# The first two attention steps of a Swin block written anew, and a convolution's pieces spread over four rounds

## The chip, the cores and the metric

The kernel runs on one core of a Trainium2 chip. The metric is the device time of one execution in microseconds (us), median of several runs. In the profile PE is TensorE, PEld its weight loads, DVE VectorE, ACT ScalarE, POOL GpSimd and SP SyncE, which only issues transfers.

## The reference

The input is 16 images of 192 channels and 56 x 56 pixels in f32. Two layers follow each other.

```python
# layer 0: a shifted-window attention block with an MLP, per image
h = layernorm(x over channels) * norm1_g + norm1_b
h = roll(h, (-3, -3))                       # then cut in 8 x 8 windows of 7 x 7
q, k, v = h @ qkv_w + qkv_b                 # 6 heads of 32 channels
p = softmax(q * 32**-0.5 @ k.T + rel_bias[REL_IDX] + window_mask)
x1 = x + roll_back(p @ v @ proj_w + proj_b)
y = gelu(layernorm(x1) @ fc1_w + fc1_b) @ fc2_w + fc2_b      # 192 -> 768 -> 192
x2 = x1 + y
# layer 1: a depthwise 3 x 3 convolution with weights made from the image itself
t  = relu(batchnorm(mean(x2 over pixels) @ w1.T))
wt = (t @ w2.T + b2) * MASK                 # of the nine taps four are not masked
out = depthwise_conv(x2, wt) + conv_bias
```

The weights of the convolution need the mean over the whole image, so it can begin only when the image's last MLP is done.

## The kernel before

A step is a quarter of an image: two bands of 7 rows, 16 windows (T = 392 pixels in a band). There are 64 steps. The kernel is software-pipelined by hand: the order written is the order on each engine. Round i (2 to 65) does the MLP of step i-2, the attention of step i, q, k and v of step i+1, and the sums for norms of steps i+2 (norm 1) and i-1 (norm 2). Steps 0 and 1 are done ahead of the rounds, in the part that is called the start here.

PSUM is taken as four pairs of banks (0 to 3), each one tile deep, so a pair is reused when the last reader of its tile is done:

```python
def banks(name, k):
    return psum.tile([128, 2, 512], F32, tag=f"pair{k}", name=name)
```

A norm is made as sums on TensorE (`st`, `singles`), a variance (`dev`), a root, a reciprocal, and then transfers that spread the result over partitions (`dv`):

```python
def norm_squares(key, i, side, engine):        # sq
    ...                                        # engine: ACT or GpSimd, two squares
    for h in range(2):
        nc.gpsimd.tensor_tensor(s0[p, h], s0[p, h], s1[p], ALU.add)

def norm_vars(keys):                           # dev <- st
    for s in sides:
        nc.scalar.activation(d[var[s]], stats[s][mean[s], :T], AF.Square)
    for s in sides:
        nc.vector.tensor_tensor(d[var[s]], stats[s][var[s], :T], d[var[s]], ALU.subtract)
...
def norm_devs(keys):
    part, d = norm_vars(keys)
    norm_root(part)                            # ACT, Sqrt
    table(AF.Gelu)                             # loads ACT's next table ahead
    nc.vector.reciprocal(part, part)
    return d
# norm_spread: dv <- dev, 8 transfers for a step; norm1_scale: win <- x * dv;
# norm2_scale: yn <- x * dv, on GpSimd
```

An attention step: scores (`sc`), `e` = scores + bias, a maximum, a subtraction, an exponential, a sum, a reciprocal, `prob` on GpSimd; then turns (`pt`, transposed on TensorE, copied to `prt` by ACT), values (`po`), rows (`o`), projection (`pp`) and residual (`x`). q, k and a mixed block e of both (`pq`, `pk`, `pe`) and v (`pv`) come from `win`; ACT copies q, k and e (`outs[0]` to `outs[3]`), DVE and ACT copy v into `vbd`.

The start, cut:

```python
... # loads of 7 rows of image 0, qkv weights, columns; then all other rows, mask, rel_bias
norm_squares("1_0", 0, 0, nc.gpsimd)
fold_scale(raw, g1, eff)
keys = stats_of(-2)                            # sums of step 0
pm = fold_means(eff, 3 * DIM, "fq", 0)
dvs.update(norm_spread(keys, norm_devs(keys), (nc.sync, nc.scalar)))
norm_squares("1_1", 1, 0, nc.gpsimd)
... # fold of qkv weights and biases; zeros into kbd, vbd, prob
keys = stats_of(-1)                            # sums of step 1
dev = norm_devs(keys)
norm1_scale(0, dvs.pop(0), nc.vector)
...
qs[0], outs = attention_qk(0, 1, 0, 2)
for f in outs:
    f()
... # image 1; proj and fc1 weights; bias_t
tail_of(-1, None, None, (2, 0))                # v of step 0
... # norm 2's parameters, fc2 weights

for i, extra in ((0, (proj_bias, mlp_weights)), (1, (taps_weights,))):
    top, share = attention_scores(i, *qs.pop(i), (1, 2, 0, 1))
    norm1_scale(i + 1, dvs.pop(0), nc.gpsimd)
    top(0)
    for wp in range(3):
        top(wp + 1)
        share(wp)
    share(3)
    qs[i + 1], outs = attention_qk(i + 1, 1, 0, 2)
    for f in outs:
        f()
    ...
    for e in extra:                            # parameters of later stages
        e()
    keys = stats_of(i)
    dev = norm_devs(keys)
    dvs.update(norm_spread(keys, dev))
    prts = [attention_turn(i, wp, wp % 2) for wp in range(4)]
    ...
    o = attention_rows(i, attention_values(i, prts, 0, 3))
    tail_of(i, o, 1, (2, 0))                   # projection, v of step i+1, residual, squares
```

The convolution of an image is six pieces (`conv_begin` on ACT, three taps on DVE in `conv_rest`, then transfers out). They are taken two in a round from the round after the image's last MLP on:

```python
for i in range(2, NS + 2):
    A, B_, C, D = pairs
    cs = conv_ready(2)
    ys = [conv_begin(*c) for c in cs[:1]]
    if has(i + 1):
        norm1_scale(i + 1, dvs.pop(0), nc.vector)
    def after():
        ys.extend(conv_begin(*c) for c in cs[1:])
        for c, y in zip(cs, ys):
            conv_rest(*c, y)
    if (i + 3) % STEPS == 0 and (i + 3) // STEPS < B:
        b = (i + 3) // STEPS
        images[b] = load_x(b, nc.sync)         # three image buffers
    def between():
        singles[0] = banks(f"st_{i}", C)
        keys.update(stats_of(i))
        var.append(norm_vars(keys))
    ...
    # ph <- yn, wf; after() runs after three of six blocks, between() after the next short ones
    mlp_first(i - 2, yns.pop(i - 2), hid, (A, B_, C, D, A, B_), after, between)
    ...
    if has(i):
        top, share = attention_scores(i, *qs.pop(i), (C, D, A, B_))
    ...
    # pf <- hid, wf, with turns, values, projection, v of step i+1, residual;
    # in each fourth round the taps of the image (taps, taps_hidden, taps_rows, taps_out)
```

Of the kernel before, what the change touches and what calls it, by code (L numbers as in the profile page):

```python
# [14 lines left out]
C0, C1 = 128, 64  # L15
# [21 lines left out]
def tile_swin_then_dynamic_conv(  # L37
# [48 lines left out]
    singles = [banks("singles", 3)]  # L86
# [44 lines left out]
    def columns(sources, tag, name, queue, k):  # L131


        n = sum(count for _, count in sources)
        rows = one.tile([n, 256], F32, tag=tag, name=f"{name}_rows")
        at = 0
        for src, count in sources:
            queue.dma_start(rows[at : at + count, 0:DIM], src.rearrange("(r c) -> r c", c=DIM))
            at += count
        nc.vector.tensor_copy(rows[:, DIM:256], rows[:, C0:DIM])  # L140
        pt = bank(k)
        for c in range(2):
            nc.tensor.transpose(
                pt[:, c * n : (c + 1) * n], rows[:, c * 128 : (c + 1) * 128], ident[:n, :n]
            )
        cols = const.tile([128, 2, n], F32, tag=name, name=name)
        nc.vector.tensor_copy(cols.rearrange("p c n -> p (c n)"), pt[:, 0 : 2 * n])
        return [(cols[:, 0, r : r + 1], cols[:, 1, r : r + 1]) for r in range(n)]
# [4 lines left out]
    def fold_scale(raw, g, dst):  # L153
        for c in range(2):
            nc.vector.tensor_scalar(dst[:, c], raw[:, c], g[c], None, ALU.mult)
# [58 lines left out]
    raw_all = one.tile([128, 2, 6 * DIM + HID], F32, tag="hid", name="raw")  # L214
    raw, eff = raw_all[:, :, 0 : 3 * DIM], raw_all[:, :, 3 * DIM : 6 * DIM]
    rawf = raw_all[:, :, 6 * DIM :]
# [24 lines left out]
    def norm_squares(key, i, side, engine):  # L241
# [9 lines left out]
        for h in range(2):  # L251
            p = slice(h * 64, h * 64 + 64)
            nc.gpsimd.tensor_tensor(s0[p, h], s0[p, h], s1[p], ALU.add)  # L253
# [22 lines left out]
    def norm_vars(keys):  # L276

        sides = sorted(keys)
        d = one.tile([128, T], F32, tag="dev", name=f"dev_{keys[sides[0]]}")
# [12 lines left out]
    def norm_devs(keys):  # L292

        part, d = norm_vars(keys)
        norm_root(part)
        table(AF.Gelu)
        nc.vector.reciprocal(part, part)
        return d

    def norm_spread(keys, d, queues=(nc.sync,)):  # L300

        out = {}
        for side in sorted(keys, reverse=True):
            tag = ("dv1", "sq01")[side]
            v = one.tile([128, 2, T], F32, tag=tag, name=f"dv_{keys[side]}")
# [40 lines left out]
    def norm2_scale(i, dv):  # L346
# [3 lines left out]
        nc.gpsimd.tensor_tensor(y0, v0, dv, ALU.mult)  # L350
        for h in range(2):
            p = slice(h * 64, h * 64 + 64)
            nc.gpsimd.tensor_tensor(y1[p], v1[p], dv[p, h], ALU.mult)
# [406 lines left out]
    def tail_of(i, o, kp, kv):  # L760

        pvs, v_rest, v_whole = attention_v(i + 1, kv) if has(i + 1) else (None, None, None)
        if o is not None:
            pp, pair1, narrow, rest, whole = project(i, o, kp, 3)
            narrow()
            rest()
        if pvs:
            v_rest()
        if o is not None:
            whole()  # L770
            residual(i, pp, pair1)
        if pvs:
            v_whole()
            attention_v_out(pvs)
        if o is not None:
            norm_squares(f"2_{i}", i, 1, nc.scalar)

# [3 lines left out]
    nc.vector.memset(pick, 0.0)  # L781
    for h in range(4):
        nc.vector.memset(pick[h * HD : (h + 1) * HD, h % 2 : h % 2 + 1], 1.0)
# [5 lines left out]
    nc.vector.memset(rel_r, 0.0)  # L789
    nc.vector.memset(wp2, 0.0)  # L790
    images[0] = new_x(0)
    load_rows(*images[0], 0, 0, WS, nc.sync)
    nc.scalar.dma_start(raw[:, 0], qkv_w[0:C0])
    rows2(raw[:, 1], qkv_w, nc.scalar)
    g1, be1, bq, bk, bv = columns(
        ((norm1_g, 1), (norm1_b, 1), (qkv_b, 3)), "q2", "cols1", nc.scalar, 0
    )
    load_rows(*images[0], 0, WS, 2 * WS, nc.sync)
    load_rows(*images[0], 0, 2 * WS, HALF, nc.sync)
    nc.sync.dma_start(mask_t, win_mask)  # L800
# [13 lines left out]
    nc.gpsimd.memset(win0, 0.0)  # L814
    nc.gpsimd.memset(win1, 0.0)
    norm_squares("1_0", 0, 0, nc.gpsimd)


    fold_scale(raw, g1, eff)
    keys = stats_of(-2)  # L820
    pm = fold_means(eff, 3 * DIM, "fq", 0)
    dvs.update(norm_spread(keys, norm_devs(keys), (nc.sync, nc.scalar)))
    norm_squares("1_1", 1, 0, nc.gpsimd)
    fold_center(eff, 3 * DIM, pm)
    for to, lo, n, s in (
        (0, 0, 128, SCALE),
        (128, DIM, 128, 1.0),
        (256, 128, 64, SCALE),
        (320, DIM + 128, 64, 1.0),
        (384, 2 * DIM, DIM, 1.0),  # L830
    ):
        nc.vector.tensor_scalar(
            wqkv[:, :, to : to + n], eff[:, :, lo : lo + n], s, None, ALU.mult
        )
    pq = bank(1)
    for c, at, lo, n, be, bias in (
        (0, 0, 0, 128, be1, bq[0]),
        (1, 0, DIM, 128, be1, bk[0]),
        (2, 0, 128, 64, be1, bq[1]),
        (2, 64, DIM + 128, 64, be1, bk[1]),  # L840
    ):
        p = slice(at, at + n)
        shift(pq[p, c : c + 1], raw, lo, n, be)
        nc.vector.tensor_tensor(qkb[p, c : c + 1], bias[p], pq[p, c : c + 1], ALU.add)
    nc.vector.tensor_scalar(qkb[:, 0:1], qkb[:, 0:1], SCALE, None, ALU.mult)
    nc.vector.tensor_scalar(qkb[0:64, 2:3], qkb[0:64, 2:3], SCALE, None, ALU.mult)
    nc.vector.tensor_scalar(kb, pick, qkb[:, 1:2], None, ALU.mult)
    for t in [kbd] + vbd + prob:
        nc.gpsimd.memset(t, 0.0)
    keys = stats_of(-1)  # L850
    dev = norm_devs(keys)
    norm1_scale(0, dvs.pop(0), nc.vector)
    dvs.update(norm_spread(keys, dev))
    norm_squares("1_2", 2, 0, nc.gpsimd)
    qs[0], outs = attention_qk(0, 1, 0, 2)
    for f in outs:
        f()
    images[1] = load_x(1, nc.sync)
    nc.gpsimd.dma_start(wp0, proj_w[0:C0])
    rows2(wp1, proj_w[:, 0:C0], nc.gpsimd)  # L860
    for h in range(2):
        p = slice(h * 64, h * 64 + 64)
        nc.gpsimd.dma_start(wp2[p, p], proj_w[C0:DIM, C0:DIM])
    nc.gpsimd.dma_start(rawf[:, 0], fc1_w[0:C0])
    rows2(rawf[:, 1], fc1_w, nc.gpsimd)
    rel_hk = rel_r[:, ::-1, :].rearrange("p k h -> p h k")
    for r in range(2):
# [14 lines left out]
    tail_of(-1, None, None, (2, 0))  # L882
    g2, be2, f2b, pb, cb = columns(
        ((norm2_g, 1), (norm2_b, 1), (fc2_b, 1), (proj_b, 1), (conv_bias, 1)),
        "sq11",
        "cols2",
        nc.gpsimd,
        0,
    )
    nc.gpsimd.dma_start(f1b, fc1_b.rearrange("(f p) -> p f", p=128))  # L890
    nc.gpsimd.dma_start(wf2, fc2_w.rearrange("(f p) n -> p f n", p=128))

    def proj_bias():

        pv = bank(1)
        for c, n in ((0, 128), (1, 64)):
            shift(pv[0:n, c : c + 1], raw, 2 * DIM + c * 128, n, be1)
            nc.vector.tensor_tensor(bv[c][0:n], bv[c][0:n], pv[0:n, c : c + 1], ALU.add)
        pv = bank(0)
        mm(pv[:, 0:1], wp0[:, 0:C0], bv[0], True, False)  # L900
        mm(pv[:, 0:1], wp1[0:64], bv[1][0:64], False, True)
        for h in range(2):
            p = slice(h * 64, h * 64 + 64)
            mm(pv[p, 1:2], wp0[:, C0:DIM], bv[0], True, False)
            mm(pv[p, 1:2], wp2[0:64, 0:64], bv[1][0:64], False, True)
        for c in range(2):
            nc.vector.tensor_tensor(pb[c], pb[c], pv[:, c : c + 1], ALU.add)

    def mlp_weights():
        fold_scale(rawf, g2, wf1)  # L910
        pm = fold_means(wf1, HID, "ff", 2)
        pf = bank(1)
        for f in range(NFC):
            shift(pf[:, f : f + 1], rawf, f * 128, 128, be2)
        fold_center(wf1, HID, pm)
        nc.vector.tensor_tensor(f1b, f1b, pf[:, :NFC], ALU.add)

    def taps_weights():

        w1n = one.tile([RED, 3, 64], F32, tag="prt", name="w1n", bufs=4)  # L920
        nc.gpsimd.dma_start(w1n, w1.rearrange("r (k c) -> r k c", c=64))
        w1d = one.tile([RED, 2, 64], F32, tag="prt", name="w1d", bufs=4)
        for h in range(2):
            nc.vector.tensor_copy(w1d[:, h], w1n[:, 2])
        pt = bank(0)
        nc.tensor.transpose(
            pt[:, 0:RED], w1n[:, 0:2].rearrange("r k c -> r (k c)"), ident[:RED, :RED]
        )
        nc.tensor.transpose(
            pt[:, 64 : 64 + RED], w1d.rearrange("r k c -> r (k c)"), ident[:RED, :RED]  # L930
        )
        nc.vector.tensor_copy(
            w1t, pt[:, 0:128].rearrange("p (k r) -> p k r", k=2)[:, :, 0:RED]
        )
        w2v = w2.rearrange("(c t) r -> c t r", t=9)[:, 0:NTAP, :]
# [238 lines left out]
```

## Time and profile before

| what | before |
|---|---|
| median of 3 runs | 3253.55 us (3251.41 to 3253.6) |
| span of the profiled run | 3251.8 us, mean granted TensorE clock 0.986 |
| PE busy | 3123.3 us (96%) |
| DVE busy | 2115.2 us (65%) |
| ACT busy | 1887.8 us (58%) |
| POOL busy | 991.6 us (30%) |
| chain that ended last | PE 85%, DVE 9%, issue 2%, POOL 1% |
| first MLP matmul (`ph`) of round 2 | 174.88 us |
| first MLP matmul of round 65, the last | 3195.77 us |

The page cuts the span in 40 slices of 81 us and gives the busy share of each engine in tenths; two slices hold the start. Windows of 20 us show it closer. Most matrix products go through one helper line (L92), so a product is known by its tiles' names: `ph` and `pf` are the MLP, `sc`, `pt`, `po`, `pp` attention, `pq`, `pk`, `pe`, `pv` q, k and v, `st` sums. The time from the first `ph` of a round to the first of the next is that round's time.

### The profile page before, as it was taken

To read this page: it belongs to the slowest core of one execution; us is meant where nothing else is said; L and a number is where in the kernel's file an instruction comes from. 1 tells how busy PE (TensorE), PEld (TensorE's weight loads), DVE (VectorE), ACT (ScalarE), POOL (GpSimd) and SP (SyncE) were. 2 spreads that over 40 slices of the span, in tenths; PEclk is the share of its full clock that TensorE was granted. 3 is DMA by queue.
4 is the path that set the end of the run, shared out by engine and by line. 5 is a ranking of instruction groups with operands and counts; after the bars stand their busy time and mean duration, and the time that the engine had idled before them with its cause. 6 is when DMAs were issued, how large, how long until landed. Compare 5 with 4: busy or idle time off the path is not lost.

```text
span 3251.8 us, 64181 instructions
## 1 busy us (share of the span) xinstructions
PE 3123.3 (96%) x26130; PEld 1937.1 (60%) x26130; DVE 2115.2 (65%) x3895; ACT 1887.8 (58%) x2988; POOL 991.6 (30%) x897
## 2 busy tenths in 40 slices
PE   5699999999999999999999999999999999999996
PEld 3556666666656656666666656666665665666653
DVE  5355675766766575685676666576676667667564
ACT  2455665655655665565565565565565666566552
POOL 5333233233223323323323323323323322322220
PEclk9699999999999999999999999999999999999998
DMA  3001011111111202112111201112111121211001
GB/s 99 16 15 51 25 37 51 37 55 31 40 52 32 60 31 61 31 31 56 36 52 40 58 26 40 51 35 56 31 37 55 31 59 32 61 30 32 22 30 45
DMA packets 79123, 135.35 MB, mean 42 GB/s; under 512 B 21766, under 2 KB 61692, under 8 KB 76908
## 3 DMA queue, kind: packets, MB, share of 16 engines
q1 hardware_dynamic: 77266, 128.54, 14.0%
q8 instruction: 206, 3.38, 0.4%
q0 software_dynamic: 1056, 1.92, 0.3%
q10 hardware_dynamic: 506, 0.79, 0.1%
q14 instruction: 89, 0.73, 0.1%
HBM read 41.25 MB, written 38.54 MB: 25 GB/s over the span
## 4 chain that ended last, share of the span: by engine, by line
PE 85%; DVE 9%; issue 2%; POOL 1%; ACT 0%; DMA 0%; SPq 0%; DVEq 0%; POOLq 0%; ACTq 0%
PE pf L92 23%; PE ph L92 19%; PE pp L92 7%; PE pv L92 6%; PE po L92 6%; PE pt L508 4%; PE pq L92 4%; PE sc L92 4%; PE pk L92 4%; PE pe L92 4%; PE st L92 3%; DVE y L708 3%; DVE win L339 1%; DVE vbd L451 1%; DVE x L584 1%
## 5 line engine op out<-in xcount | busy, mean ns | idle before, releaser
L92 PE MATMUL ph<-yn,wf 128*128 128x392 f32 (+1 forms) x3072 | 808.8, 501 | 9.3 <-ACT hid L598 3.5
L92 PE MATMUL pf<-hid,wf 128*128 128x392 f32 (+1 forms) x3072 | 802.8, 494 | 3.5 <-ACT hid L598 2.0
L495 POOL TENSOR_TENSOR prob<-e,tot 113x588 f32<-113x588 f32 x256 | 298.6, 1177 | 1205.6 <-DVE tot L494 1190.0
L92 PEld LDWEIGHTS ph<-yn,wf 128*128 128x128 f32 (+1 forms) x3072 | 424.7, 188 | 365.0 <-issue 83.9
L451 ACT COPY vbd<-pv 49x192 f32<-49x192 f32 x512 | 160.6, 314 | 704.2 <-DVE vbd L451 699.5
L92 PEld LDWEIGHTS pf<-hid,wf 128*128 128x128 f32 (+1 forms) x3072 | 386.3, 164 | 303.7 <-issue 120.0
L644 DVE SCALAR_TENSOR_TENSOR x<-pf,cols,x 128x784 f32<-128x784 f32 (+1 forms) x128 | 106.1, 829 | 537.8 <-PE pf L92 508.7
L598 ACT ACTIVATE hid<-ph,f1b 128x784 f32<-128x784 f32 x384 | 337.2, 913 | 115.1 <-PE ph L92 114.0
L253 POOL TENSOR_TENSOR sq<-sq,sq 64x392 f32<-64x392 f32 x256 | 263.7, 1030 | 369.5 <-ACT sq L247 354.9
L708 DVE SCALAR_TENSOR_TENSOR y<-x,wt,y 128x770 f32<-128x770 f32 x288 | 314.0, 1104 | 16.6 <-ACT y L693 8.4
L350 POOL TENSOR_TENSOR yn<-x,dv 128x784 f32<-128x784 f32 x64 | 119.0, 1859 | 571.3 <-DMA dv<-dev 549.1
L92 PEld LDWEIGHTS pv<-wqkv,win 64*128 64x128 f32 (+1 forms) x2048 | 258.1, 190 | 35.1 <-ACT kbd L405 2.8
L92 PE MATMUL pv<-wqkv,win 64*128 64x192 f32 (+1 forms) x2048 | 274.8, 327 | 3.3 <-ACT kbd L405 2.5
L486 DVE TENSOR_TENSOR e<-e,top 113x588 f32<-113x588 f32 x256 | 267.1, 1043 | 8.9
L92 PE MATMUL pp<-o,wp 128*128 128x392 f32 (+2 forms) x896 | 251.5, 514 | 2.7 <-ACT o L544 2.7
L489 ACT ACTIVATE e<-e 113x588 f32<-113x588 f32 x256 | 176.7, 691 | 132.9 <-DVE e L486 132.9
L238 ACT ACT_TABLE_LOAD x192 | 246.3, 1283 | 3.4
L514 ACT COPY prt<-pt 128x678 f32<-128x678 f32 x256 | 179.3, 727 | 117.2 <-PE pt L508 115.7
L479 DVE TENSOR_TENSOR e<-sc,bias_t 113x588 f32<-113x588 f32 x256 | 179.9, 763 | 100.5 <-PE sc L92 100.3
L508 PEld LDWEIGHTS pt<-ident,prob 113*128 113x128 f32 x1536 | 167.3, 142 | 77.8 <-issue 48.7
L92 PE MATMUL po<-prt,vbd 128*64 128x49 f32 x6144 | 199.9, 225 | 0.0
L92 PEld LDWEIGHTS po<-prt,vbd 128*64 128x64 f32 x6144 | 191.9, 140 | 9.4 <-ACT prt L514 0.6
(146 smaller groups left out, 3987.0 us busy)
## 6 DMA issues: line engine op xcount, KB each, us to landing
dv<-dev SPq DMA_DIRECT2D x1020, 49.0 KB
x<-in_x_dram SPq DMA_DIRECT2D x15, 1484.0 KB
out_dram<-y SPq DMA_DIRECT2D x48, 392.0 KB
out_dram<-y SPq DMA_DIRECT2D x48, 196.0 KB
x<-in_x_dram SPq DMA_DIRECT2D x16, 392.0 KB
x<-in_x_dram SPq DMA_DIRECT2D x15, 350.0 KB
out_dram<-y SPq DMA_DIRECT2D x16, 308.0 KB
out_dram<-y SPq DMA_DIRECT2D x16, 154.0 KB
```

Of the source, the lines that this page charges most:

```text
L92: nc.tensor.matmul(dst, lhs, rhs, start=start, stop=stop, skip_group_check=True)
L238: nc.scalar.activation(junk, eps_t[0:1], func)
L253: nc.gpsimd.tensor_tensor(s0[p, h], s0[p, h], s1[p], ALU.add)
L451: copy(dst, src[s * 64 : s * 64 + N, h, :, :, j, :])
L479: nc.vector.tensor_tensor(e, sc[:PW, :, : HEADS * N], rel, ALU.add)
L486: nc.vector.tensor_tensor(ehs[wp], ehs[wp], t.broadcast_to([PW, 2 * HEADS, N]), ALU.subtract)
L489: nc.scalar.activation(es[wp], es[wp], AF.Exp)
L495: nc.gpsimd.tensor_tensor(prob[wp][:PW, :, 0:N], ehs[wp], t.broadcast_to([PW, 2 * HEADS, N]), ALU.mult)
L508: nc.tensor.transpose(pt[:, a, g * PW : (g + 1) * PW], prob[wp][:PW, h : h + 2, :].rearrange("p h k -> p (h k)"), ident[:PW, :PW],)
L514: nc.scalar.copy(prt, pt[:, :, : 3 * PW])
L598: nc.scalar.activation(hid[:, f], phs[f][:, :, :T], AF.Gelu, bias=f1b[:, f : f + 1])
L708: nc.vector.scalar_tensor_tensor(dst, src, wt[:, kc, t : t + 1], dst, ALU.mult, ALU.add)
```

## The change

The start is written anew, straight and without the loop. It is to bring everything in order of need:

- parameter rows are loaded first on ACT's queue, fc1's weights follow the image on SyncE's, proj weights and norm 2's rows come early on GpSimd's; the taps' parameters are loaded in the start rather than when they are used;
- qkv weights are scaled straight into their place instead of through a copy; zeros go in on DVE early;
- squares of step 0 and 1 go to ACT, the adds of step 0 to DVE; steps 1 and 2 get their sums together, step 3 with norm 2 of step 0;
- v of step 0 follows q and k of step 0 at once; q and k of step 1 are issued before the maxima of step 0; the proj bias moves to the beginning, fc1's fold into step 0, fc1's shifts and the taps' parameters into step 1;
- ACT's tables are loaded ahead of need.

In the rounds, an image's six pieces are taken 1, 2, 2, 1 over four rounds instead of 2, 2, 2 over three, and in round 64 `yn` is made half by DVE. The order of bank pairs is named otherwise.

```diff
-    singles = [banks("singles", 3)]
+    singles = [None]
...
-    def norm_squares(key, i, side, engine):
+    def norm_squares(key, i, side, engine, adder=None):
...
-            nc.gpsimd.tensor_tensor(s0[p, h], s0[p, h], s1[p], ALU.add)
+            (adder or nc.gpsimd).tensor_tensor(s0[p, h], s0[p, h], s1[p], ALU.add)
...
+    table(AF.Sqrt)
+    g1, be1, bq, bk, bv = columns(*rows1, 2)
+    norm_squares("1_0", 0, 0, nc.scalar, nc.vector)
+    fold_scale(raw, g1, wqkv, (...))
+    singles[0] = banks("st_a", 3)
+    keys = {0: "1_0"}
+    norm_stats(keys, {0: 0})
+    part, dev = norm_vars(keys, "o")
+    norm_root(part)
+    nc.vector.reciprocal(part, part)
+    dvs.update(norm_spread(keys, dev, (nc.sync, nc.scalar)))
+    pm = fold_means(wqkv, 3 * DIM, "fq", 0)
+    fold_center(wqkv, 3 * DIM, pm)
...                                            # qkv biases
+    norm_squares("1_1", 1, 0, nc.scalar)
+    norm_squares("1_2", 2, 1, nc.gpsimd)
+    singles[0] = banks("st_b", 3)
+    keys = {0: "1_1", 1: "1_2"}
+    norm_stats(keys, {0: 1, 1: 2})
...                                            # norm 2's columns, proj bias
+    part, dev = norm_vars(keys)
+    norm_root(part)
+    norm1_scale(0, dvs.pop(0), nc.vector)
+    nc.vector.reciprocal(part, part)
...                                            # rel_bias, mask, spread, image 1
+    norm_squares("1_3", 3, 0, nc.gpsimd)
...                                            # loads of later parameters
+    qs[0], outs = attention_qk(0, 1, 2, 3)
+    pvs, v_rest, v_whole = attention_v(0, (0, 1))
+    v_rest()
+    v_whole()
+    table(AF.Exp)
+    for f in outs:
+        f()
...                                            # bias_t
+    fold_scale(rawf, g2, wf1, ((0, 0, HID, 1.0),))
+    attention_v_out(pvs)
+    top, share = attention_scores(0, *qs.pop(0), (3, 2, 0, 1))
+    norm1_scale(1, dvs.pop(0), nc.gpsimd)
...
+    pm = fold_means(wf1, HID, "ff", 2)
+    qs[1], outs = attention_qk(1, 0, 3, 1)
+    top(0)
+    for wp in range(3):
+        top(wp + 1)
+        share(wp)
+    share(3)
+    outs[0]()
+    outs[1]()
+    fold_center(wf1, HID, pm)
+    prts = [attention_turn(0, wp, (0, 2)[wp % 2]) for wp in range(4)]
+    outs[2]()
+    outs[3]()
+    pos = attention_values(0, prts, 1, 0)
+    o = attention_rows(0, pos)
+    pvs, v_rest, v_whole = attention_v(1, (2, 3))
+    v_rest()
+    v_whole()
+    attention_v_out(pvs)
+    norm1_scale(2, dvs.pop(1), nc.vector)
+    pp, pair1, p_narrow, p_rest, p_whole = project(0, o, 1, 0)
...
+    residual(0, pp, pair1)
+    norm_squares("2_0", 0, 1, nc.scalar)
+
+    top, share = attention_scores(1, *qs.pop(1), (2, 3, 0, 1))
+    qs[2], outs = attention_qk(2, 2, 3, 0)
+    singles[0] = banks("st_c", 1)
+    keys = {0: "1_3", 1: "2_0"}
+    norm_stats(keys, {0: 3, 1: 0})
+    top(0)
+    top(1)
+    share(0)
+    outs[0]()
+    top(2)
+    share(1)
+    outs[1]()
+    part, dev = norm_vars(keys)
+    top(3)
+    share(2)
+    share(3)
+    table(AF.Sqrt)
+    norm_root(part)
+    nc.vector.reciprocal(part, part)
+    dvs.update(norm_spread(keys, dev, (nc.sync, nc.gpsimd)))
...
+    table(AF.Gelu)
+    pf = banks("f1b_p", 2)[:, 0]
+    for f in range(NFC):
+        shift(pf[:, f : f + 1], rawf, f * 128, 128, be2)
+    nc.vector.tensor_tensor(f1b, f1b, pf[:, :NFC], ALU.add)
+    prts = [attention_turn(1, wp, (0, 2)[wp % 2]) for wp in range(4)]
+    outs[2]()
+    outs[3]()
+    yns[0] = norm2_scale(0, dvs.pop(1), True)
+    norm_squares("1_4", 4, 0, nc.gpsimd)
+    pos = attention_values(1, prts, 3, 0)
+    o = attention_rows(1, pos)
+    pvs, v_rest, v_whole = attention_v(2, (1, 2))
...                                            # v, projection, residual, taps' parameters
-    pairs = [0, 1, 3, 2]
+    pairs = [0, 3, 1, 2]
...
-        cs = conv_ready(2)
+        cs = conv_ready(1 if convs and not convs[0]["n"] else 2)
...
-            yns[i - 1] = norm2_scale(i - 1, dvs.pop(1))
+            yns[i - 1] = norm2_scale(i - 1, dvs.pop(1), i == NS)
```

## The prediction

> **What bounds the kernel now.** I read the page's slices first, then 20 us windows of the start, then the chain of waits, then the timelines of two rounds.
>
> ```profile
> PE   5699999999999999999999999999999999999996
> PEclk9699999999999999999999999999999999999998
> ```
>
> TensorE is full in all but the first two slices (81 us each) and the last: the rounds are TensorE's, and only time at which it stands still can be taken from them. The start, by windows (PE, PEld, DVE, ACT, POOL busy, granted clock, DMA):
>
> ```profile
> 80.00:100.00 20.00, 18.21 (x61) 11.40 (x61) 3.91 (x11) 5.54 (x9) 2.08 (x2) 0.50 0.00 0
> 100.00:120.00 20.00, 15.30 (x165) 12.77 (x164) 5.72 (x10) 7.87 (x12) 4.31 (x4) 0.83 0.08 21
> 140.00:160.00 20.00, 11.05 (x100) 7.61 (x100) 5.78 (x13) 13.72 (x20) 5.81 (x11) 0.78 0.27 31
> 200.00:220.00 20.00, 20.00 (x193) 13.12 (x192) 9.38 (x14) 10.78 (x18) 7.70 (x8) 1.00 0.16 41
> ```
>
> Up to 175 us no engine is full and the clock is often half: a chain of waits. From 200 us PE has 20.00 of 20. The chain that ended last shows what it waits for (start, us, what):
>
> ```profile
> 104.58 20.66 issue
> ...
> 145.26 4.94 DMA bn<-in_L_conv_beta_dram
> ...
> 174.88 10.03 PE ph L92 x36
> ...
> 224.50 8.10 PE ph L92 x36
> ```
>
> GpSimd stands still for 20.66 us in step 0 because the squares of the next sum come last; late parameter loads hold step 1; and round 2, the first with an MLP, begins at 174.88. Its first 36 ph records take 10.03 us against 8.10 a round later.
>
> Last, round 6 (conv pieces begin) and round 7 on PE, and round 6 on DVE:
>
> ```profile
> 374.99 1.73 PE L92 MATMUL ph<-yn,wf 64*128 64x392 f32 x8 [0.23 <-ACT hid L598]
> ...
> 384.53 2.24 PE L92 MATMUL sc<-kbd,q 64*64 64x98 f32 x96 [1.54 <-DVE dev L285]
> ```
>
> ```profile
> 432.20 2.24 PE L92 MATMUL sc<-kbd,q 64*64 64x98 f32 x96
> ```
>
> ```profile
> 370.42 0.19 DVE L657 COPY x<-x 128x56 f32<-128x56 f32 x1
> ...
> 377.03 6.18 DVE L708 SCALAR_TENSOR_TENSOR y<-x,wt,y 128x770 f32<-128x770 f32 x6
> 383.24 1.14 DVE L285 TENSOR_TENSOR dev<-st,dev 64x392 f32<-64x392 f32 x2
> ```
>
> In round 6 DVE first makes the taps (370.42 to 372.39), then two pieces, and only then the subtraction that frees the bank of the scores: PE waits 1.54 us. In round 7 the same matmuls follow without a wait. Rounds start with the first ph: 367.81, 417.75, 465.43, so round 6 takes 49.94 us and round 7 47.68. Rounds 10, 14, ... 58 repeat 49.94; round 62 is like them.
>
> **What the Trainium skill says.** "TensorE: Matmul & The Clock Gate", Part 1 (What's actually happening): TensorE's default is half clock, and a window of sustained work releases it. The trace agrees: granted 0.50 from 80 to 100 us, 1.00 once the rounds run. "ScalarE: Activation LUTs", What ACT_TABLE_LOAD costs: 1283 ns for any table; here 192 loads of 1283 ns mean. "SBUF — State Buffer", Who interferes with whom: VectorE and GpSimd share a port pair that one holds for a whole instruction. Here the subtraction of the maximum takes 0.77 to 1.31 us according to whether GpSimd multiplies beside it, and two win multiplies took 2.58 us in round 6 against 1.05 alone.
>
> **The change part by part.** All times after are my estimates: start plus durations, and each instruction waits for its inputs, for its bank, and for what stands ahead of it on its engine. Durations and times not shown in a fence are those of the single engines' timelines over the first 175 us.
>
> *Up to q and k of step 0.* Image rows come as before (GpSimd's first square started at 12.61). ACT squares 0.86+0.51, DVE adds about 0.9 in place of GpSimd's 2.08: 14.9. Sums 2.6 (the row at 16.03), 17.5; ACT 0.49, DVE 0.57, root 0.62 without its 1.28 table load, reciprocal 2.60: 21.8 (before 23.72). ACT's four spread issues (0.6 each) hold it to 24.3, its squares of step 1 to 25.7, GpSimd's adds 2.08 to 27.8, its squares of step 2 1.49+0.84+2.08 to 32.2; last sums 1.3, proj bias 2.3 and adds to 36.7; subtractions 1.14, win 3.13: 41.0. Before, PE's q began at 44.23. This serial path is why the beginning gains only 3. q, k, e take 8.8 at the cold clock, as before (44.23 to 52.99): 49.8.
>
> *v and scores of step 0.* v now has banks 0 and 1 and nothing to wait for: 1.47+2.76 as in a warm round, 54.0 (before it waited for the copies of k and ended at 63.50). Its eight DVE copies 2.94 partly beside it, then four score adds of 0.93: 58.8, before 69.95. Gain 11.
>
> *Rest of step 0.* The chain of maxima and sums keeps 10.65 us: 69.7. Before, the turns began only at 99.95: 19.4 us for proj bias, the fc1 fold, 24 cold shifts (6.23) and sums stood ahead of them on PE. Now fold means lie under the chain, shifts wait for step 1. ACT, after the last exponential at 68.9: copies of q and k 2.8, to 71.7; four turns through two banks, each a transpose and a copy of 0.73, to 74.7; copies of e 3.5, to 78.2. Values (3.0) lie under these; v needs that bank, 3.5: 81.7; vbd 2.2, win of step 2 3.1, residual 2.2: 89.2, before 119.59. Gain 30.
>
> *Step 1.* Adds 3.1: 92.3; two maxima, a share, a maximum, a share 6.8: 99.1. Then DVE waits: q and k of step 2 reach PE only as the score banks come free, the sums end near 100.5, ACT squares 1.0, subtractions: 102.9. Last maximum and two shares 3.9: 106.8; beside it table and root to 107.7; reciprocal 110.3. The second turn needs the bank of the fc1 shifts, which DVE empties after that: two rounds of transpose and copy through that bank, to 113.4. Values use the bank of e: copies 3.5, 116.9. Values cold 4.5, v 4.2, projection 3.9: 129.5. I add 2.5 for small waits: round 2 at 132, before 174.88. **Gain 43.**
>
> *Spread pieces.* One piece (half of 6.18) leaves round 6, so the subtraction ends at 381.3, before ph ends on PE at 378.76+4.22 = 383.0: the 1.54 vanish. The rest of round 6's excess, 0.23 and slower ph, comes from taps and vbd copies, which stay. Rounds 6, 10, ... 62 are 15: **23.** The fourth round gets the piece: rounds 7 and 8 hide two.
>
> *Round 2 and tail.* With v and projection without a break PE should be warm: 1.8 of round 2 go, but the second ph block waits for a residual just done, about 0.7: 1. Near the end PE waits 2.26 for GpSimd's yn; halved between two engines, about 0.9. Sum 43+23+1+1 = 68, 3185.5. I put 3187, since a chain set out by hand rather omits waits than invents them.
>
> **Rivals.** (1) The freed DVE slot in round 6 moves no end, because ACT's gelu or vbd becomes the last releaser: gain 45, 3208. For it: the 0.23 wait on hid. Against: the 1.54 names DVE dev, and DVE would be 1.7 us early. (2) The fourth round costs what the first saves. The image load three later reuses buffers whose last piece now lies in that round, and the load stands ahead of the spread transfers in one queue: 13 loads by 1 to 2 us, 3200 to 3213. Against: only the last rows (x1) are still held, the piece ends some 9 us in, and spreads are issued 33 us in. (3) Step 1 stays a chain: bank waits and cold clock eat the reordering, round 2 at 145: 3200. For it: every bank I traced there is reused within 5 us. (4) The start overlaps better than I let it, round 2 at 122: 3177.
>
> **Range and chances.** Round 2's start carries most: plus 8 or minus 8 us; the pieces 15 to 34 (34 if round 6's whole 2.26 goes). Together 3175 to 3200. Two per cent is 3188.5, which my sum passes by 1.5 to 3: 0.56 faster, 0.43 same. A slowdown of 65 us would need a stall of 4 us in each fourth round: 0.01.
>
> **What would show it.** First ph near 132 (right: 125 to 138). Score adds of step 0 done near 59, its residual near 89. A DVE gap before dev in step 1. Round 6 about 48.4 without a wait on DVE dev before sc; rounds 7 and 9 still 47.7 and 48.1. If round 9 is longer than 48.5, rival 2; if round 6 stays above 49, rival 1. Wrong altogether if steady rounds 7 and 8 change, where nothing is altered.

## The result and the profile after

| | before | after |
|---|---|---|
| median | 3253.57 us (3251.41 to 3254.99) | 3179.86 us (3179.02 to 3180.44) |
| ratio, 95% interval | | 0.9774 [0.9757, 0.9791] |
| span of the profiled run, clock | 3251.8 us, 0.986 | 3177.7 us, 0.992 |
| first `ph` of round 2 | 174.88 | 129.02 |
| rounds 6, 10, ... 58 | 49.94 each | 48.33 each (round 10: 48.43) |
| round 62, 63 | 49.27, 40.92 | 47.65, 41.27 |
| round 64, 65 (to the end) | 29.90, 56.07 | 27.57, 54.76 |
| rounds 7, 8 and 5, 9 | 47.68 and 48.12 | 47.68 and 48.12 |

The kernel became 2.3% faster, and the whole interval lies under 0.98. From the rows of the table the 74.1 us by which the span fell come out as: start 45.9, pieces 14 x 1.61 + 1.62 = 24.2, round 2 1.3 (49.45 to 48.19), tail -0.35 + 2.33 + 1.31 = 3.3; together 74.6. The 0.5 between them is rounding and what rounds 10 and 40 took more than so counted, 0.1 and 0.3.

The slices of the page after:

```profile
PE   7899999999999999999999999999999999999996
PEclk9899999999999999999999999999999999999998
```

Only the first two slices are left below 9 before the tail. The start by 20 us windows (PE, PEld, DVE, ACT, POOL busy, granted clock, DMA):

```profile
80.00:100.00 20.00, 18.73 (x183) 11.07 (x182) 17.09 (x40) 9.41 (x18) 4.37 (x4) 0.99 0.01 2
100.00:120.00 20.00, 10.47 (x102) 9.64 (x102) 8.00 (x12) 10.83 (x18) 12.60 (x16) 0.50 0.17 40
140.00:160.00 20.00, 20.00 (x163) 12.24 (x164) 15.99 (x23) 16.71 (x24) 4.65 (x4) 1.00 0.01 2
200.00:220.00 20.00, 20.00 (x193) 13.18 (x191) 9.94 (x14) 11.34 (x19) 7.75 (x7) 1.00 0.16 38
```

From 80 to 100 us PE now works 18.73 of 20 us at full clock. One window is still a chain of waits, 100 to 120: PE 10.47, clock 0.50. The steady window from 200 on is as it was. What the hole consists of, the chain of waits says (start, us, what):

```profile
103.60 1.28 ACT L245
105.67 2.48 issue
108.41 3.65 PE pt L514 x18
...
116.31 4.74 PE po L92 x96
121.05 4.30 PE pv L92 x32
125.35 3.85 PE pp L92 x14
...
130.78 7.02 PE ph L92 x32
```

After a table load (L245) and the reciprocal (the 2.48 of "issue") come the last three turns, ACT's copies of e, the values, v, projection, and the MLP of round 2. The last line answers to the 10.03 us of before: from the first `ph` at 129.02 to 137.80 it is 8.78 now, which is round 2's gain.

Round 6 on PE after; the 1.54 us of waiting before `sc` is gone:

```profile
320.69 6.95 PE L92 MATMUL ph<-yn,wf 128*128 128x392 f32 x28
327.87 1.73 PE L92 MATMUL ph<-yn,wf 64*128 64x392 f32 x8 [0.23 <-ACT hid L604]
...
335.79 2.24 PE L92 MATMUL sc<-kbd,q 64*64 64x98 f32 x96
```

The same round on DVE:

```profile
329.90 3.13 DVE L714 SCALAR_TENSOR_TENSOR y<-x,wt,y 128x770 f32<-128x770 f32 x3
333.07 1.14 DVE L292 TENSOR_TENSOR dev<-st,dev 64x392 f32<-64x392 f32 x2
```

Three taps where there were six; the subtraction ends at 334.21, and `ph` ends on PE at 331.65 + 4.22 = 335.87. DVE is 1.66 us early.

### The profile page after: what moved, and what is told of

Its sections match the earlier page's. It is cut to its first block, busy times and chain, and to the rows that moved or that the text cites. A ratio compares the mean times of both kernels' runs of the same rounds, so it can differ in the third digit from the quotient of the medians.

```text
span 3177.7 us, 64151 instructions
## 1 busy us (share of the span) xinstructions
PE 3106.6 (98%) x26130; PEld 1923.3 (61%) x26130; DVE 2132.4 (67%) x3916; ACT 1879.4 (59%) x2984; POOL 973.0 (31%) x880
## 3 DMA queue, kind: packets, MB, share of 16 engines
q0 software_dynamic: 1168, 1.54, 0.3%
## 4 chain that ended last, share of the span: by engine, by line
PE 92%; DVE 4%; ACT 3%; issue 1%; DMA 0%; POOL 0%; ACTq 0%; SPq 0%; DVEq 0%; POOLq 0%
PE pf L92 24%; PE ph L92 22%; PE pp L92 8%; PE pv L92 7%; PE po L92 6%; PE pq L92 5%; PE pt L514 5%; PE sc L92 4%; PE st L92 4%; PE pk L92 4%; PE pe L92 4%; DVE vbd L457 1%; DVE x L590 1%; ACT hid L604 0%; ACT vbd L457 0%
## 5 line engine op out<-in xcount | busy, mean ns | idle before, releaser
L714 DVE SCALAR_TENSOR_TENSOR y<-x,wt,y 128x770 f32<-128x770 f32 x288 | 327.2, 1146 | 16.8 <-ACT y L699 8.2
L457 DVE COPY vbd<-pv 49x192 f32<-49x192 f32 x512 | 181.3, 354 | 30.8 <-PE pv L92 23.6
```

What stands on the lines that cost most here:

```text
L457: copy(dst, src[s * 64 : s * 64 + N, h, :, :, j, :])
L714: nc.vector.scalar_tensor_tensor(dst, src, wt[:, kc, t : t + 1], dst, ALU.mult, ALU.add)
```

## The experiments

My theory going in: start, pieces and tail are separate gains, each from one named wait; what is left of round 6 and of the start's hole has causes that can be removed singly. The rivals were that the parts need each other, that the fourth piece round costs something, and that the rest of the hole is the clock's.

### Are start and pieces separate gains?

Two kernels, each with one part: the pieces alone in the kernel before, and the kernel after with the pieces again 2, 2, 2.

```diff
 # e1, from before
-        cs = conv_ready(2)
+        cs = conv_ready(1 if convs and not convs[0]["n"] else 2)
 # e2, from after
-        cs = conv_ready(1 if convs and not convs[0]["n"] else 2)
+        cs = conv_ready(2)
```

> The kernel before with one edit: pieces 1, 2, 2, 1 over four rounds; its start is left as it was. Theory (in round 6 DVE makes the taps and two pieces before the subtraction that frees the scores' bank, 1.54 us of PE): rounds 6, 10, ... 62 go from 49.94 to 48.33, round 9 stays 48.12, round 2 still begins at 174.9; 15 x 1.61 = 24, about 3229.5. Rival (the rounds gain only because the new start numbers the bank pairs otherwise): rounds stay at 49.94, 3253.

> The changed kernel with the pieces back at 2, 2, 2. Theory: the parts add, round 2 begins at 129.0, rounds 6, 10, ... go back to 49.94, about 3204. Rival (start and pieces share a gain, the PE clock or a bank): less than 20 or more than 28 us is lost.

| | pieces 2, 2, 2 | pieces 1, 2, 2, 1 |
|---|---|---|
| start and tail before | 3252.83 | 3227.49 (0.9923 [0.9908, 0.9938]) |
| start and tail after | 3207.65 (0.9861 [0.9847, 0.9876]) | 3179.86 (0.9774 [0.9757, 0.9791]) |

The pieces bring 25.3 alone and 27.8 beside the new start. Round 6 doesn't depend on the start ahead of it: 48.33 in the first kernel as in the kernel after, 49.93 in the second against 49.94 before; round 9 is 48.12 in all four. So the parts add up, and the difference between 25.3 and 27.8 is within the intervals (0.15% of 3250 is 5 us). In the second kernel's profiled run, rounds 18, 22 and 54 took 52.01, 51.63 and 51.15 us instead of 49.93, 5.0 together, with gaps on PE in rounds 22 and 54 that no wait explains; that alone is more than the difference. What this doesn't show is how the 46 us of the start divide among its many edits.

### What is left of round 6?

Round 6 is still 0.65 above round 7. The prediction put it down to taps and copies of v. The rival is the piece that stayed. The kernel after with no piece in the first round of an image (0, 2, 2, 2):

```diff
+        n0 = convs[0]["n"] if convs and "wt" in convs[0] else None
+        fresh = n0 == 0 and not convs[0].get("held")
+        if fresh:
+            convs[0]["held"] = True
-        cs = conv_ready(1 if convs and not convs[0]["n"] else 2)
+        cs = conv_ready(0 if fresh else 2)
```

> The changed kernel with no piece in the first round after an image and 2, 2, 2 in the next three. Theory: one piece already fits before the scores, so nothing more is won there on DVE; what ACT's first pass of the piece costs, the 0.23 us wait on hid, goes (48.33 to 48.1), and the fourth round hides two pieces, since DVE had 1.69 us idle before dev and 1.8 us after it: about 3176. Rival (the fourth round is full: two late pieces and a later image load): round 9 grows by 1 to 2 us over 48.12, 15 times, 3190 to 3205.

3170.64 us, 0.9751 [0.9736, 0.9766]. Round 6 takes 47.68, like round 7, with taps and copies of v still in it; round 9, now with two pieces, stays 48.12. The reason is on ACT, in the kernel after:

```profile
325.85 1.03 ACT L699 ACTIVATE y<-x,cols,wt 128x784 f32<-128x784 f32 x1
326.90 2.52 ACT L604 ACTIVATE hid<-ph,f1b 128x784 f32<-128x784 f32 x3
```

The first step of the piece (`y`, 1.03 us) stands ahead of the gelu (`hid`) that frees a bank for `ph`. Without it, on ACT:

```profile
326.81 0.51 ACT L254 ACTIVATE sq<-x 128x392 f32<-128x392 f32 x1
327.35 2.53 ACT L604 ACTIVATE hid<-ph,f1b 128x784 f32<-128x784 f32 x3
```

and on PE:

```profile
322.07 8.26 PE L92 MATMUL ph<-yn,wf 128*128 128x392 f32 x36
```

Counted from the round's first `ph`, the gelu begins after 5.28 us (327.35 - 322.07) instead of 6.21 (326.90 - 320.69), and the 36 `ph` run through in 8.26 us instead of 327.87 + 1.73 - 320.69 = 8.91: the 0.65. Fifteen of these are 9.8 us; the medians differ by 9.2.

### Does the tail's gain come from the halved `yn`?

The tail brought 3.3 where 0.9 had been predicted. The kernel after with `yn` whole on GpSimd in round 64:

```diff
-            yns[i - 1] = norm2_scale(i - 1, dvs.pop(1), i == NS)
+            yns[i - 1] = norm2_scale(i - 1, dvs.pop(1))
```

> The changed kernel with yn of round 64 on GpSimd alone again (the start's own use of both engines stays). Theory: round 64 to 65 waits 2.26 us for yn again, and the gap lets the PE clock fall for a window, about 1.1 more in round 65: 3183. Rival (the shorter last rounds come from the pieces, one of which moved out of the end): no change, 3180.

3183.6 us, 0.9789 [0.9773, 0.9806]; round 64 takes 30.15 and round 65 55.87, near the 29.90 and 56.07 of the kernel before. The last `ph` on PE, here:

```profile
3126.19 14.18 PE L92 MATMUL ph<-yn,wf 128*128 128x392 f32 x48 [2.51 <-POOL yn L355]
```

and in the kernel after:

```profile
3122.94 0.93 PE L92 MATMUL ph<-yn,wf 128*128 128x392 f32 x2
3124.17 11.86 PE L92 MATMUL ph<-yn,wf 128*128 128x392 f32 x46 [0.31 <-POOL yn L353]
```

DVE's half lets PE begin two matmuls early, so the wait is 0.31 instead of 2.51, and the 48 matmuls take 0.93 + 11.86 = 12.79 instead of 14.18. The second effect is the clock: in the kernel before it was granted 0.5 for 3.41 us from 3196.02, right after the wait (in e4 from 3126.16); after, it stays at 1.0 up to 3154.61, behind the last product of the MLP. There a short wait cost its length and 1.4 us on top.

It doesn't always. e1 has the tail of the kernel before, and PE waits nearly as long:

```profile
3171.70 12.52 PE L92 MATMUL ph<-yn,wf 128*128 128x392 f32 x48 [2.06 <-POOL yn L350]
```

Here the grant stays at 1.00 (3171 to 3190), the 48 matmuls take 12.52, and rounds 64 and 65 take 29.70 and 53.89, 1.3 more than in the kernel after instead of 3.6. So 1.3 us of the gain came without the clock; whether the clock falls behind such a wait varies, and what decides it isn't shown.

### Can the first chain be shortened on GpSimd?

Up to the first win the start is one serial chain: norm of step 0, spread, squares of steps 1 and 2, sums. GpSimd idles early, so e5 gives it the squares of steps 2 and 1 at once:

```diff
+    norm_squares("1_2", 2, 1, nc.gpsimd)     # before the weights are scaled
+    norm_squares("1_1", 1, 0, nc.gpsimd)     # after the sums of step 0
...
-    norm_squares("1_1", 1, 0, nc.scalar)     # after the spread
-    norm_squares("1_2", 2, 1, nc.gpsimd)
```

> The changed kernel with the squares of steps 1 and 2 on GpSimd as soon as its rows are there (step 2 first), in place of ACT after its spread transfers. Theory (the beginning is one serial path: reciprocal, ACT's transfer issues, ACT squares, GpSimd adds and squares, sums): the sums of steps 1 and 2 end about 3 us earlier, after the qkv bias shifts on PE at 27.2, win of step 0 at 37.4 in place of 40.4, and round 2 about 3 us earlier, 126: 3177. Rival (step 0 is held by the spread of its own norm or by later loads): the beginning does not move, 3180.

Four kernels with one and the same start (after, e2, e3, e4) began round 2 at 129.02, 129.86, 130.40 and 130.16 in their profiled runs. Counted from ACT's first square, which waits for the image, it is 115.73 to 116.48 us. From here on I give this distance too; a difference below 0.8 in it says nothing.

3183.23 us, 0.9785 [0.977, 0.9799]; round 2 at 130.77, 117.02 from the first square: the 3 us of the theory did not come, and up to 1.3 may have been lost; the interval overlaps that of the kernel after. First and last group of the ten weight scales on DVE, after:

```profile
15.78 0.48 DVE L163 TENSOR_SCALAR wqkv<-raw,cols 128x128 f32<-128x128 f32 x2
...
16.89 0.87 DVE L161 TENSOR_SCALAR wqkv<-raw,cols 128x64 f32<-128x64 f32 x4
```

and in e5:

```profile
16.24 2.21 DVE L163 TENSOR_SCALAR wqkv<-raw,cols 128x128 f32<-128x128 f32 x2
...
20.60 2.74 DVE L161 TENSOR_SCALAR wqkv<-raw,cols 128x64 f32<-128x64 f32 x4
```

17.76 - 15.78 = 2.0 us became 23.34 - 16.24 = 7.1, while GpSimd squared and added from 15.67 to 25.28. The reciprocal behind the scales ended at 27.22 instead of 21.73, and the sums at 34.13 instead of 33.53 (from the first square 20.38 and 20.24): the squares made early gained nothing. "SBUF — State Buffer", Who interferes with whom, in the Trainium skill lists `tensor_scalar` among the VectorE operations that can take the shared pair and then contend with GpSimd; this trace agrees, with a factor of 3.6.

The same squares can go to ACT, behind the root and ahead of its spread issues; e10 does that, on top of two edits described below:

```diff
     norm_root(part)
+    norm_squares("1_1", 1, 0, nc.scalar)
+    norm_squares("1_2", 2, 1, nc.scalar)
     nc.vector.reciprocal(part, part)
 ...                                          # both cut from behind the spread
```

> As e9, and both squares of steps 1 and 2 are made by ACT between root and spread (19.1 to 21.8), so GpSimd only adds, after DVE has folded the weights. Theory (GpSimd's multiplies beside the fold held DVE's scales 7.1 us in place of 2.0 in e5, and that alone spoilt it): the fold keeps 2.0 us, the sums end at about 31 in place of 33.5, win of step 0 and everything after 2.5 us earlier: round 2 at about 121, 3162.5. Rival (another chain holds win of step 0, such as the transfers of its norm): unchanged, 3165.

3163.24 us, 0.9721 [0.9706, 0.9735]. The scales take 2.0 us again, the sums end at 31.20, win of step 0 at 38.5 instead of 40.4, and round 2 begins at 121.03, 2.7 before the same kernel without the edit (e9, 123.74); from the first square it is 107.85 against 110.28. That the chain was the limit stands; the engine I gave its work to first was the wrong one.

### What holds the end of step 1?

In the hole from 102 to 116 us two waits stand behind each other: the last turns wait for the fc1 shifts' bank, the values for ACT's copies of e. On PE after:

```profile
97.22 4.61 PE L92 MATMUL f1b_p<-cols,raw 128*128 128x1 f32 x24
...
108.41 3.63 PE L514 MATMUL pt<-ident,prob 113*128 113x113 f32 x18 [5.26 <-DVE f1b L996]
116.31 4.74 PE L92 MATMUL po<-prt,vbd 128*64 128x49 f32 x96 [4.27 <-ACT kbd L411]
```

e6 removes the first: the shifts go into a gap of PE at 35 us. e7 removes the second: the copies of e go from behind the turns to ahead of the last maximum, where ACT idles. e8 has both and e5's edit.

```diff
 # e6: after the proj bias
+    pf = banks("f1b_p", 0)[:, 0]
+    for f in range(NFC):
+        shift(pf[:, f : f + 1], rawf, f * 128, 128, be2)
 ...                                          # add after bias_t; both cut from step 1
 # e7
     part, dev = norm_vars(keys)
+    outs[2]()
+    outs[3]()
     top(3)
 ...
     prts = [attention_turn(1, wp, (0, 2)[wp % 2]) for wp in range(4)]
-    outs[2]()
-    outs[3]()
```

> The changed kernel with the 24 fc1 shifts moved from step 1 into PE's wait for win of step 0 (35.2 to 40.4). Theory: q and k of step 0 start on a warmer clock (8.7 us down to 7 to 8), and the second turn of step 1 no longer waits for the reciprocal and the bank of the shifts (108.4), so turns end near 110.5 and values start near 114 in place of 116.3; round 2 at about 125.5, 3176. Rival (step 1 is bound by ACT's table loads and copies, not by that bank): round 2 moves by 1 us or less for it, 3179.

> The changed kernel with ACT's copies of e of step 2 (3.5 us) ahead of the last maximum of step 1, where ACT is idle, in place of after the turns. Theory (values of step 1 wait for the bank of e): values start right after the last turn's copy, 112.8 in place of 116.3; the delayed last exponential costs up to 0.8: round 2 at about 126, 3177. Rival (the norm's root behind them on ACT becomes later by as much): 3180 or more.

e6: 3179.87 us, 0.9774 [0.976, 0.9789], like the kernel after; round 2 at 128.43, 114.89 from the first square, 0.8 to 1.6 less than with the unchanged start, where 3.5 were expected. Its PE in step 1:

```profile
108.42 2.49 PE L514 MATMUL pt<-ident,prob 113*128 113x113 f32 x12 [6.81 <-ACT prt L520]
115.19 5.27 PE L92 MATMUL po<-prt,vbd 128*64 128x49 f32 x96 [4.28 <-ACT kbd L411]
```

The wait for the bank went to another releaser at the same time, 108.42: the turns' first copy stands on ACT behind two table loads and the exponential that DVE feeds. At the front, PE's gap was filled, and q, k and e still took 8.5 us up to v (8.7 in the kernel after). Here the Trainium skill differs from the trace: "TensorE: Matmul & The Clock Gate", Part 1 (What's actually happening), gives about 3.4 us of sustained work for full clock. The gap was filled with 5.8 us of one-column matmuls back to back:

```profile
33.94 1.51 PE L92 MATMUL pb_p<-cols,wp 128*128 128x1 f32 x12
35.38 4.33 PE L92 MATMUL f1b_p<-cols,raw 128*128 128x1 f32 x24
```

Yet the grant was 0.5 from 38.29, in their midst, to 45.12, against 38.24 to 45.07 without the shifts: here they didn't count as such work.

e7: 3174.22 us, 0.9758 [0.9741, 0.9774], round 2 at 123.36, 5.7 earlier, and 110.17 from the first square. PE in step 1:

```profile
108.82 3.62 PE L514 MATMUL pt<-ident,prob 113*128 113x113 f32 x18 [7.57 <-DVE f1b L998]
112.37 3.01 PE L92 MATMUL po<-prt,vbd 128*64 128x49 f32 x96
```

The turns come 0.4 later, but the values follow them without a wait: 116.31 - 112.37 = 3.94 us, and they run in 3.01 instead of 4.74 because the clock is back just before they start (half from 102.06 to 112.30; after, from 99.68 to 120.16). That is 5.67 together. In the kernel after ACT had room for these copies just there:

```profile
102.89 0.69 ACT L495 ACTIVATE e<-e 113x588 f32<-113x588 f32 x1 [2.74 <-DVE e L492]
```

ACT idles 2.74 us ahead of the last exponential; in e7 the copies (3.6 us, 99.68 to 103.26) lie there and delay it to 103.30, by 0.4.

> The three edits together. Theory: they lie on one chain after another and add, and the second turn is free as well: values of step 1 at about 106, round 2 at about 119: 3170. Rival (yn of step 0 becomes the bound: reciprocal, spread, two multiplies): round 2 at 122 or later, 3173.

e8: 3176.3 us, 0.9762 [0.9748, 0.9777], round 2 at 125.97, 111.52 from the first square: no better than e7 alone, and not clearly worse, since the intervals overlap. Step 1's sums end at 99.68 against 96.79 in e7. Of these 2.9 us, 1.26 are the image's rows, which came later (first square at 14.45 and 13.19), and 1.0 is q, k and e of step 0, which took 9.20 us instead of 8.22 on a clock that was back at 48.00 instead of 44.03; e5's edit can account for the rest.

### What becomes of them together?

e9 joins e3 and e7; e10, shown above, adds the squares on ACT; e11 adds e6's shifts to e10 and moves the Gelu table load behind the rows of step 1, so that the turns' copies come earlier.

```diff
 # e11, on e10 with e6's edit
-    table(AF.Gelu)
     prts = [attention_turn(1, wp, (0, 2)[wp % 2]) for wp in range(4)]
 ...
     o = attention_rows(1, pos)
+    table(AF.Gelu)
```

> The changed kernel with pieces 0, 2, 2, 2 and with the copies of e of step 2 early. Theory: the two lie in different parts and add, 9.2 + 5.6: round 2 at 123.4, round 6 at 47.68, about 3165. Rival (a shorter start moves the rounds' DMA or clock): 3168 or more.

> As e10, and the fc1 shifts in PE's wait for win of step 0, and ACT's load of the Gelu table after the rows of step 1 in place of ahead of the turns. Theory (e6 won little because the turns of step 1 then waited for ACT, which had two tables to load first): the turns start 1.5 us earlier, and without the shifts' bank they end about 3.5 us earlier: round 2 at about 117.5, 3159. Rival (yn of step 0 or the cold clock takes over): 1 us or less.

| | us | ratio to before | round 2 at |
|---|---|---|---|
| e9 | 3165.82 | 0.9729 [0.9713, 0.9745] | 123.74 |
| e10 | 3163.24 | 0.9721 [0.9706, 0.9735] | 121.03 |
| e11 | 3160.05 | 0.9713 [0.9699, 0.9728] | 122.52 |

All three beat both kernels; by their intervals neighbours in the table can't be told apart. In e11's profiled run the image's rows came 1 us later (ACT's first square at 14.19, in e10 at 13.18), so I compare from the end of step 1's sums to round 2: 25.45 us (97.07 to 122.52) against 26.57 in e7, 26.36 in e10 and about 31.7 in the kernel after. The turns' last copy ended 2.5 earlier than in e7 (110.67 for 113.21), but:

```profile
109.84 4.70 PE L92 MATMUL po<-prt,vbd 128*64 128x49 f32 x96
```

4.70 for 3.01: the values now start before the clock is back (113.60; in e7 it was 112.30, just ahead of them), and more than half of the gain goes there. The rest went ahead of the sums: from the first square to their end e11 took 82.88 us and e10 81.49, most of it in q, k and e of step 0 (9.13 instead of 7.84, the clock back at 45.34 instead of 41.50). From the first square to round 2 e11 is at 108.33, e10 at 107.85: in these two runs e11's edits gained nothing.

### Would the fold have been better in step 0?

The change puts fc1's shifts in step 1. e12 puts means and shifts between q, k of step 1 and the turns of step 0, where PE waits as well; the shifts share the means' tile.

```diff
-    pm = fold_means(wf1, HID, "ff", 2)
     qs[1], outs = attention_qk(1, 0, 3, 1)
+    pm = fold_means(wf1, HID, "ff", 2)
+    for f in range(NFC):
+        shift(pm[:, 0, 400 + f : 401 + f], rawf, f * 128, 128, be2)
 ...                                          # cut from step 1
```

> The changed kernel with fc1's fold means and shifts put back on PE between q, k of step 1 and the turns of step 0, as the kernel before had them. Theory (PE's order, not its work, made step 0 long): turns of step 0 end about 3 us later, values follow, v of step 1 and all after it about 3 us later; step 1 gains about 1 back, as its second turn has its bank: round 2 at 131 to 132, 3182. Rival (ACT's copies bind step 0 in any case): round 2 at 129 or earlier, 3180.

3185.15 us, 0.979 [0.9775, 0.9805]; round 2 at 136.2, 7.2 later, and 122.96 from the first square, 6.5 to 7.2 more. The turns of step 0 start at 75.29 instead of 68.82, because the shifts fill PE up to there. The direction is shown. The size is partly my edit's: with one tile, the centring of fc1 on DVE had to wait for the shifts too, and the copies of e ended at 85.31 instead of 77.35; and the values of step 0 ran at half clock (73.05 to 83.29), 4.03 us instead of 3.01. The second turns of step 1 waited again for ACT (7.67 us), as in e6.

## Why the prediction was right

The time came out 7 us under the 3187 predicted and in the range; the line of 2%, 3188.5, to which it gave a chance of 0.56, is passed by 8.6 us.

**Start: 43 predicted, 45.9 measured.** The chain set out by hand ended at 129.5, and 2.5 were added for small waits: the measured 129.02 shows none left to add (129.86 to 130.40 in e2, e3 and e4). This addition and the tail's 2.4 are the largest parts of the error; a second allowance, 1.5 from 3185.5 to 3187, comes next. Its stations:

| station | predicted | measured |
|---|---|---|
| spread of step 0 issued | 24.3 | 24.55 |
| win of step 0 | 41.0 | 40.4 |
| q, k, e of step 0 | 49.8 | 49.08 |
| score adds of step 0 | 58.8 | 58.11 |
| copies of e, step 0 | 78.2 | 77.35 |
| residual of step 0 | 89.2 | 87.98 |
| subtraction of step 1's norm | 102.9 | 101.32 |
| reciprocal | 110.3 | 108.24 |
| last turn's copy | 113.4 | 112.81 |
| copies of e, step 1 | 116.9 | 116.26 |
| projection, round 2 | 129.5 | 129.02 |

Errors are 0.3 to 2.1 us and don't add up; at the end 0.5 is left. The DVE gap ahead of the subtraction, named as a sign, is there: 2.70 us, released by ACT's square. The order held: q, k, e cold at 8.7 us; shares, turns and copies as set out; the bank of the shifts emptied only after the reciprocal. Two terms were too small: win of step 0 took 3.90 us instead of 3.13, and from the reciprocal to the last turn's copy it was 4.57 instead of 3.1, since three turns, not two, stand behind it (their copies start at 109.81, 110.94 and 112.08). The other stretches, up to 1.5 too long, made up for it: that only 0.5 remained is partly luck. One sum is off, 58.8 + 10.65 = 69.45 and not 69.7; it does no harm.

**Pieces: 23 predicted, 24.2 measured**, by the mechanism named: the subtraction 1.66 early where 1.7 was said, no wait before `sc`, rounds 7, 8 and 9 unchanged. One statement beside it failed: "The rest of round 6's excess, 0.23 and slower ph, comes from taps and vbd copies, which stay." It came from the piece that stayed, on ACT ahead of the gelu (e3), and it need not have stayed. The error hid in the total since only the size of what stays mattered there.

**Round 2: 1 predicted, 1.26 measured.** PE is warm (granted 1.0 from 120.16 on), and the wait for the residual is 0.28 instead of the 0.7 allowed.

**Tail: 0.9 predicted, 3.3 measured.** The mechanism was right, the term mis-sized: "halved between two engines" took half of the wait, but one half is enough to begin, so the wait fell from 2.26 to 0.31; and the clock's fall behind the wait (14.21 to 12.79 us for the same matmuls) wasn't counted at all. That the profiled run of the kernel before had this fall is partly luck: in e1, behind 2.06 us, it did not come.

**The clock.** The prediction reads the half clock from 80 to 100 us of the kernel before as agreement with the page it cites. Its own line doesn't fit that: PE is busy 18.21 of these 20 us, 6.35 of them in eight `ff_m` back to back (84.43 to 90.78), and the clock comes back only at 100.13. No term of the sum rests on it.

**The rivals.** (1) fell: nothing else became the last releaser in round 6 at the old place; 0.65 remain, and not from the gelu's own wait but from what stands before it. (2) fell in its cost, not in its event: the load of the image's last rows did wait for the piece,

```profile
474.30 0.52 SPq L103 DMA_DIRECT2D x<-in_x_dram  x1
```

15 us after the load before it (in the kernel before it followed at once, 508.66 after 508.19), and round 9 still took 48.12, since the spreads behind it were due only at 495.62. (3) had one point: step 1 did stay a chain from 101 to 116, at half clock; but it was in the sum already, and round 2 didn't come at 145. (4), 122, didn't come by the change, but with e7's two moved lines (123.36) and e10's squares (121.03).

What stays open: how e11 and e10 rank; what e12 would cost with a tile of its own for the shifts; and what each edit in the start is worth, since only the place of the fc1 fold was tried singly.

## What to carry to other kernels

The start of a software-pipelined kernel is one chain: set it out from measured durations, with each engine's order and each bank's last reader, and give each turn through a bank its own term; here it came out within 0.5 us of 129 without an allowance, with some help from errors that cancelled. Then ask of every wait in it what stands ahead of the releaser on its engine: two calls moved on ACT were worth 5.7 us, one piece held back from a crowded round 9 us, while work moved to an idle engine (GpSimd) or an idle gap of PE brought no gain in the medians (e5, e6). And count a wait of TensorE with what may follow it: matmuls behind it ran at half clock, which made a wait of 2.3 us cost 3.7 and one of 4 us cost 5.7; behind one of 2.06 us in e1 they ran at full clock. Last, before reading a difference of 1 us in a start, see how far kernels with the same start differ: here 1.4 us, and 0.8 from the first square.

## What the runs showed of the hardware unexpectedly

- Weight scales on VectorE (`tensor_scalar`, 128 x 128, f32) took 0.24 us each alone and up to 1.1 beside two-input multiplies on GpSimd: ten of them 2.0 and 7.1 us.
- One-column matmuls, 36 in 5.8 us back to back, didn't keep TensorE's clock: it fell to half in their midst (e6, 38.29). Eight matmuls of 384 columns, 6.35 us back to back, didn't bring it back either (kernel before, 84.43 to 90.78).
- The recorded grant can read 1.0 ahead of its first recorded change although matmuls run at half speed: in the kernel before it does so up to 55.76 us, yet the first four `pq` of step 0, at 44.23, took 1.88 us, and the same four 0.93 in round 6.
- A table load of 1.28 us was followed by the next instruction on ACT without further delay: loaded from 103.60 to 104.88, next start 104.89 in the kernel after.
